# First tokens loaded ahead of the branch, the flag computed first, and the feed-forward normalized a step earlier

## The chip, the cores and the metric

The kernel runs on one core of a Trainium2 chip. The metric is the device time of one execution in microseconds. Before the change it is 2756.72 us, the median of three executions (2755.34 to 2758.24).

The core has five instruction queues that matter here: TensorE (PE in the profile, its weight loads PEld), VectorE (DVE), ScalarE (ACT), GpSimd (POOL) and SyncE (SP), which here does nothing but issue DMAs. Each works through its instructions in the order of the program and waits at semaphores.

## What is computed

The input `x` has the shape (2, 256, 128, 128): batch, time, band, channel. A block of three residual parts is applied, all in float32:

```python
xt = _ln(x, ln_t_w, ln_t_b).transpose(0, 2, 1, 3)
x = x + _mha(xt, t_wi, t_bi, t_wo, t_bo, H_T, cm).transpose(0, 2, 1, 3)   # over time, causal
xf = _ln(x, ln_f_w, ln_f_b)
x = x + _mha(xf, f_wi, f_bi, f_wo, f_bo, H_F, bm)      # over bands, |i - j| <= 16
xn = _ln(x, ln_n_w, ln_n_b)
h = jax.nn.gelu(xn @ w1.T + b1, approximate=False)     # 512 hidden channels
x = x + (h @ w2.T + b2)
```

`_ln` is a layer norm over the 128 channels, `_mha` an attention of four heads of 32 channels.

## The kernel before

**Prologue.** `load_constants` (L39) issues the loads of the columns of constants and the rows of biases on SP, and the six weights on ACT's DMA queue. `fold` (L335) then folds the layer norms' scales into the weights (`wf`, `w1f`), works out the biases (`bq`, `orow`, `b1`), and computes from the weights' norms a flag that says whether the scores are small enough to take exponentials without subtracting the maximum. Every engine reads the flag (L423) and branches (L1118). `bounded_path` is the branch that is taken here; `shifted_path` is the other. Matmuls of `fold` write to PSUM tiles that one pool holds; VectorE does all the elementwise work. The scheduler orders the instructions of `fold`.

**Groups.** After the branch all work is cut into groups of four tiles of 128 tokens (512 tokens of 128 channels). There are 128 groups of attention over time (`OverTime`), and then sixteen runs, each of 8 groups of attention over bands (`OverBands`) and 8 of the feed-forward (`FeedForward`) on the same tokens. Four groups share a quad, a tile `x` of four DMAs of 256 KB. There are four such buffers. Attention over time writes its sum to a tensor `x1` in DRAM, from which the bands' groups load; the bands' sum stays on the chip as `x2`, where the feed-forward reads it.

**What a group goes through.** `statistics` (mean and variance, on VectorE), a reciprocal root (`rstd`), `normalize` (VectorE writes `xh`, four instructions), `turn` (VectorE transposes 32x32 blocks into `z`, and four DMAs write it to a DRAM tile `turned`), `fetch` (one DMA of 256 KB reads it back as `xnT`, channels on partitions), and then the products. In the attentions these are `qp`, `kp`, `vp`, the scores `sp`, the sums `rp` and `op`, and the output `yp`; in the feed-forward `hp` (four products of 128x512, in two halves) and `zp`.

**The pipeline.** `run` writes one step per group index `n`, and in each step the parts of several groups that are at different stages. `do_at(n + 3, OverTime, "fetch")` says that in step `n` group `n + 3` is fetched if it is one over time. The order of PE, VectorE, ACT and POOL is kept as it is written (`InOrder`); SP's is not, and a scheduler puts its DMAs in order by what it reckons to be ready. The lines that matter:

```python
        for n in range(-11, len(groups) + 2):
            do(n + 11, "load")
            do_at(n + 3, OverTime, "fetch")
            do_at(n + 2, OverBands, "fetch")
            do_at(n + 1, FeedForward, "fetch")
            do_at(n + 2, FeedForward, "normalize", "turn")
            do_at(n + 3, OverBands, "normalize", "turn")
            do_at(n + 4, OverTime, "normalize", "turn")
```

So the bands' groups are normalized three steps ahead and fetched two, the feed-forward's two and one. The tiles `xnT` have three buffers, `xh` and `z` two, `turned` three. The first `load`s stand in eleven steps in which nothing else happens yet; they issue two DMAs of a quad at a time. DMAs share eight semaphores, and one that takes a semaphore waits for the DMA that had it before.

Of the kernel before, what the change touches and what calls it, by code (L numbers as in the profile page):

```python
# [10 lines left out]
F32 = mybir.dt.float32  # L11
# [8 lines left out]
P = 128  # L20
# [18 lines left out]
def load_constants(ctx, tc, x, t_wiT, t_woT, f_wiT, f_woT, w1T, w2T, cols, rows):  # L39
    nc = tc.nc  # L40
    B, T, FB, C = x.shape
    k = Consts()
    k.NI = w1T.shape[1] // P
    const = ctx.enter_context(tc.tile_pool(name="const", bufs=1))
    k.const = const
    k.cols = const.tile([P, 16], F32, name="cols_sb")
    nc.sync.dma_start(k.cols, cols)
    k.rows = const.tile([P, 3, C], F32, name="rows_sb")
    for i in range(3):
        nc.sync.dma_start(k.rows[:, i, :], rows[i : i + 1, :].partition_broadcast(P).squeeze(1))  # L50
# [284 lines left out]
def fold(tc, k):  # L335

    nc = tc.nc
    const = k.const  # L340
    C = P
    scale = 1.0 / math.sqrt(D)

    def col(i):
        return k.cols[:, i : i + 1]
# [3 lines left out]
    k.wf, k.wn, k.bq, k.orow = [], [], [], []  # L349
    tests = const.tile([P, 6], F32, name="tests")  # L350
    with tc.tile_pool(name="foldp", bufs=2) as fp, tc.tile_pool(name="foldps", bufs=1, space=PSUM) as pp:
        for a in range(2):
            c0 = 5 * a
            wi, wo = k.wiT[a], k.woT[a]

            bp = pp.tile([P, 2], F32, name="bp")
            nc.tensor.matmul(bp[:, 0:1], wi[:, 0:C], col(c0 + 1), start=True, stop=True)
            nc.tensor.matmul(bp[:, 1:2], wi[:, 2 * C : 3 * C], col(c0 + 1), start=True, stop=True)
            bq = const.tile([P, 1], F32, name=f"bq{a}")
            nc.vector.tensor_scalar(bq, bp[:, 0:1], col(c0 + 2), scale, ALU.add, ALU.mult)  # L360
            bv = fp.tile([P, 1], F32, name="bv")
            nc.vector.tensor_tensor(bv, bp[:, 1:2], col(c0 + 4), ALU.add)
            wf = const.tile([P, 3 * C], F32, name=f"wf{a}")
            nc.vector.tensor_scalar(wf[:, 0:C], wi[:, 0:C], col(c0), scale, ALU.mult, ALU.mult)
            nc.vector.tensor_scalar(wf[:, C : 3 * C], wi[:, C : 3 * C], col(c0), None, ALU.mult)
            wn = const.tile([P, C], F32, name=f"wn{a}")
            nc.vector.tensor_scalar(wn, wo, -1.0, None, ALU.mult)

            bvb = fp.tile([P, P], F32, name="bvb")
            nc.vector.tensor_scalar(bvb, k.ones, bv, None, ALU.mult)  # L370
            op = pp.tile([P, C], F32, name="op")
            nc.tensor.matmul(op, bvb, wo, start=True, stop=True)
            orow = const.tile([P, C], F32, name=f"orow{a}")
            nc.vector.tensor_tensor(orow, op, k.rows[:, a, :], ALU.add)

            brp = pp.tile([1, P], F32, name="brp")
            nc.tensor.matmul(brp, bq, k.ident, start=True, stop=True)
            br = fp.tile([1, P], F32, name="br")
            nc.vector.tensor_copy(br, brp)
            gq = pp.tile([P, P], F32, name="gq")  # L380
            nc.tensor.matmul(gq, wf[:, 0:C], wf[:, 0:C], start=True, stop=False)
            nc.tensor.matmul(gq, br, br, start=False, stop=True)
            gk = pp.tile([P, P], F32, name="gk")
            nc.tensor.matmul(gk, wf[:, C : 2 * C], wf[:, C : 2 * C], start=True, stop=True)
            gs = fp.tile([P, P], F32, name="gs")
            nc.vector.tensor_copy(gs, gq)
            nc.vector.tensor_tensor(gs, gk, gs, ALU.mult)
            for h in range(H):
                r = slice(h * D, (h + 1) * D)
                nc.vector.tensor_reduce(tests[r, 3 * a : 3 * a + 1], gs[r, r], AX.X, ALU.add)  # L390
            for j, w in ((1, wf[:, 2 * C : 3 * C]), (2, wo)):
                sq = fp.tile([P, P], F32, name="sq")
                nc.vector.tensor_tensor(sq, w, w, ALU.mult)
                nc.vector.tensor_reduce(tests[:, 3 * a + j : 3 * a + j + 1], sq, AX.X, ALU.add)
            k.wf.append(wf)
            k.wn.append(wn)
            k.bq.append(bq)
            k.orow.append(orow)
        b1p = pp.tile([P, k.NI], F32, name="b1p")
        for j in range(k.NI):  # L400
            nc.tensor.matmul(
                b1p[:, j : j + 1], k.w1T[:, j * P : (j + 1) * P], col(11), start=True, stop=True
            )
        k.b1 = const.tile([P, k.NI], F32, name="b1")
        nc.vector.tensor_tensor(k.b1, b1p, k.cols[:, 12 : 12 + k.NI], ALU.add)
        k.w1f = const.tile([P, k.NI * P], F32, name="w1f")
        nc.vector.tensor_scalar(k.w1f, k.w1T, col(10), None, ALU.mult)

        tp = pp.tile([P, 6], F32, name="tp")
        nc.tensor.matmul(tp, k.ones, tests, start=True, stop=True)  # L410
        ok = fp.tile([P, 6], F32, name="ok")
        for a in range(2):
            nc.vector.tensor_scalar(
                ok[:, 3 * a : 3 * a + 1], tp[:, 3 * a : 3 * a + 1], SAFE * SAFE / (C * (C + 1)), None, ALU.is_le
            )
            nc.vector.tensor_scalar(
                ok[:, 3 * a + 1 : 3 * a + 3], tp[:, 3 * a + 1 : 3 * a + 3], LARGE, None, ALU.is_le
            )
        allok = fp.tile([P, 1], F32, name="allok")
        nc.vector.tensor_reduce(allok, ok, AX.X, ALU.min)  # L420
        flag = const.tile([P, 1], I32, name="flag")
        nc.vector.tensor_copy(flag, allok)
    return nc.values_load(flag[0:1, 0:1], min_val=0, max_val=1)  # L423


# [451 lines left out]
class BoundedPath:  # L877
# [53 lines left out]
    def groups(self, x, out):  # L931
# [3 lines left out]
        for b in range(B):  # L935
            for f0 in range(0, FB, GA):
                held = {}


                def load(g, f0=f0, b=b, held=held):  # L940
                    if g == 0:
                        self.quad(held, "x", 4)
                    for i in range(2 * g, min(2 * g + 2, NT)):
                        f = f0 + i // NC_T * NT
                        nc.sync.dma_start(held["x"][rows_of(i)], self.of_times(x[b], i, slice(f, f + NT)))

                def store(g, f0=f0, b=b, held=held):
                    for i in range(NT if g % 2 else 0):
# [14 lines left out]
        for b in range(B):  # L963
            for r0 in range(0, T, RUN):
                run = []
                for t0 in range(r0, r0 + RUN, GB):
# [3 lines left out]
                    def load(g, t0=t0, b=b, held=held):  # L970
                        if g == 0:
                            self.quad(held, "x", 4)
                            self.quad(held, "x2", 2 * RUN // GB)
                        for i in range(2 * g, min(2 * g + 2, NT)):
                            nc.sync.dma_start(
                                held["x"][rows_of(i)].rearrange("q g t c -> q (g t) c"),
                                self.of_bands(k.x1[b], t0 + NT * i, NT),
                            )
# [18 lines left out]
                for g, part, _, store in run:  # L997
                    yield FeedForward(self, partial(part, "x2", g), partial(part, "res", g), None, partial(store, g))

    def run(self, x, out):  # L1000
        groups = list(self.groups(x, out))

# [12 lines left out]
        A = RUN // NT  # L1015

        self.scalar.preload_act_table_set(EXP_SET)
        for n in range(-11, len(groups) + 2):
            feeds = [at(n - 2 + i, FeedForward) for i in range(5)]
            bands = [at(n - 2 + i, OverBands) for i in range(5)]  # L1020
            turn = feeds[2] and bands[1]
            old, new = (groups[i] if at(i, OverTime) else None for i in (n, n + 1))
            self.by_columns = at(n - 1, Attention)
            do(n + 11, "load")
            if bands[2] and feeds[1]:
                self.scalar.preload_act_table_set(EXP_SET)
            do_at(n + 4, FeedForward, "root")
# [131 lines left out]
```

## Time and profile before

| | |
|---|---|
| median of three executions | 2756.72 us |
| the profiled execution | 2757.78 us |
| its span, first to last instruction | 2755.9 us |
| granted TensorE clock, mean | 0.997 |
| PE idle at the start, up to 40.88 us | 3.45, 1.49 and 25.77 us |
| PE idle after its last matmul | 8.1 us |
| DMA, mean over the span | 125 GB/s |

Busy time says how long an engine worked; a wait says for what it stood idle and how long. In a row of the timeline the numbers are the start in us from the span's start, the time to the end of the last instruction of the row, the engine, the line, the operation, the tile it writes and what it reads, and the idle time before it with what ended it. Almost every instruction has the line L872, that of the helper that records it, so rows are told apart by their tiles. A matmul of float32 stands as two records. An `issue` row of SP (SPq) is the time that the issuing took, not that of the transfer.

The stretches of the start, in the view by windows (busy us and instructions of each engine, granted clock, share of the DMA engines' time, GB/s):

```profile
0.00:16.50 16.50, 10.18 (x38) 8.01 (x38) 8.81 (x46) 0.00 (x0) 0.69 (x6) 1.00 0.25 76
16.50:23.50 7.00, 0.00 (x0) 0.00 (x0) 0.06 (x1) 1.28 (x1) 0.79 (x3) 1.00 0.87 199
23.50:41.00 17.50, 0.12 (x1) 0.15 (x1) 12.07 (x56) 1.51 (x6) 0.00 (x0) 1.00 0.91 202
```

In the first the fold runs, in the second all engines stand while the DMA engines are 87% busy, in the third VectorE alone works.

### The profile page before, as it was taken

Reading aid. Unit: us, or ns where it says so; the run is one execution under the profiler, and the core shown is the slowest. Engines: PE = TensorE matmul, PEld = TensorE weight load, DVE = VectorE, ACT = ScalarE, POOL = GpSimd, SP = SyncE. Lnnn points to the kernel's source line nnn. Section 1 sums busy time; section 2 is a strip of 40 time slices with the busy share of each in tenths; the row PEclk is TensorE's granted clock in tenths of the full one; section 3 lists DMA queues with packets and bytes.
Section 4 is the critical chain, followed back from the end, with each engine's and each line's share of the span. In section 5 each row is a group of like instructions: output and inputs, shape, how many; then the busy total and the mean of one; then the engine's idle time right before and its main releaser. Section 6 shows DMA issues by size and latency. Waiting matters only on the chain.

```text
span 2755.9 us, 105739 instructions
## 1 busy us (share of the span) xinstructions
PE 2695.7 (98%) x43522; PEld 1880.6 (68%) x43522; DVE 2288.9 (83%) x6727; ACT 1843.3 (67%) x3600; POOL 1861.0 (68%) x2169
## 2 busy tenths in 40 slices
PE   5999999999999999999999999999999999999998
PEld 3666766667666666676676766766766767667666
DVE  5999999999999987868778778687687796776874
ACT  3888888888888874655746646557456465465563
POOL 2878878788887876666657566666566665665762
PEclk9999999999999999999999999999999999999999
DMA  5565555555555564444443544544444445344333
GB/s 126 135 154 135 148 156 141 142 154 144 148 149 144 134 157 105 109 129 108 121 127 105 129 108 109 132 115 115 129 107 122 111 114 130 103 117 113 87 97 86
DMA packets 471310, 343.84 MB, mean 125 GB/s; under 512 B 43296, under 2 KB 405152, under 8 KB 470816
## 3 DMA queue, kind: packets, MB, share of 16 engines
q1 hardware_dynamic: 469568, 335.92, 47.3%
q8 instruction: 344, 5.64, 0.9%
q14 instruction: 150, 1.23, 0.2%
q10 hardware_dynamic: 1248, 1.05, 0.1%
HBM read 169.03 MB, written 167.77 MB: 122 GB/s over the span
## 4 chain that ended last, share of the span: by engine, by line
PE 82%; DVE 11%; DMA 4%; issue 1%; SPq 1%; POOL 1%; ACT 0%; DVEq 0%
PE zp L872 17%; PE hp L872 16%; PE sp L872 10%; PE op L872 7%; PE rp L872 7%; PE vp L872 7%; PE qp L872 6%; PE kp L872 6%; PE yp L872 6%; DVE xh L872 2%; DVE vy L872 2%; DMA xnT<-turned 2%; DVE u L872 1%; DVE stats L872 1%; DVE res L872 1%
## 5 line engine op out<-in xcount | busy, mean ns | idle before, releaser
L872 ACT ACTIVATE hT<-hp,b 128x512 f32<-128x512 f32 x512 | 350.2, 687 | 553.0 <-PE hp L872 542.1
L872 POOL TENSOR_SCALAR_AFFINE_SELECT pf<-pf 128x512 f32<-128x512 f32 x768 | 476.9, 635 | 274.8 <-ACT pf L872 248.6
L872 DVE TENSOR_SCALAR xh<-x,mv,rstd 128x160 f32<-128x160 f32 x1536 | 596.2, 430 | 14.1
L872 PEld LDWEIGHTS zp<-w2T_sb,hT 128*128 128x128 f32 x4096 | 476.3, 192 | 56.2 <-issue 54.1
L872 PE MATMUL hp<-xnT,w1f 128*128 128x512 f32 x1024 | 471.2, 597 | 13.5 <-DMA xnT<-turned 11.6
L872 PE MATMUL zp<-w2T_sb,hT 128*128 128x128 f32 x4096 | 479.8, 275 | 0.1
L872 ACT ACTIVATE p<-sp 128x512 f32<-128x512 f32 (+1 forms) x1024 | 417.3, 501 | 19.9 <-PE sp L872 7.5
L872 POOL TENSOR_SCALAR_AFFINE_SELECT p<-p 128x1024 f32<-128x1024 f32 x256 | 280.2, 1095 | 199.9 <-ACT p L872 199.8
L872 PE MATMUL sp<-qT,kT 32*128 32x128 f32 (+1 forms) x8192 | 363.0, 310 | 5.4 <-DVE oT L872 3.6
L872 PEld LDWEIGHTS sp<-qT,kT 32*128 32x128 f32 x8192 | 310.7, 185 | 56.7 <-ACT kT L872 44.4
L872 PEld LDWEIGHTS vp<-wf,xnT 128*32 128x32 f32 (+1 forms) x7400 | 237.9, 113 | 153.8 <-issue 137.8
L872 POOL TENSOR_TENSOR p<-p,p 128x512 f32<-128x512 f32 x256 | 328.7, 1284 | 10.7
L872 DVE BATCH_NORM_STATS2 stats<-x 128x6 f32<-128x128 f32 x1536 | 327.6, 276 | 6.9 <-DMA x<-in_x 6.8
L872 PEld LDWEIGHTS hp<-xnT,w1f 128*128 128x128 f32 x1024 | 182.3, 191 | 191.4 <-issue 115.3
L872 ACT ACTIVATE pf<-sp 128x512 f32<-128x512 f32 x512 | 264.3, 603 | 59.2 <-PE sp L872 59.0
L872 PE MATMUL qp<-xnT,wf 128*32 128x512 f32 (+1 forms) x1850 | 267.2, 593 | 27.8 <-DMA xnT<-turned 25.8
L872 DVE STREAM_TRANSPOSE z<-xh 128x512 f32<-128x512 f32 x384 | 273.3, 712 | 15.6 <-DMA turned<-z 2.2
L872 POOL TENSOR_SCALAR rstd<-mv 128x4 f32<-128x4 f32 x248 | 56.3, 227 | 331.9 <-DVE mv L872 330.8
L872 ACT ACTIVATE qT<-qp,bq 128x512 f32<-128x512 f32 x256 | 176.0, 687 | 146.0 <-PE qp L872 146.0
L872 PE MATMUL vp<-wf,xnT 128*32 128x128 f32 (+1 forms) x7400 | 272.3, 273 | 0.0
L872 POOL TENSOR_TENSOR rstd<-rstd,mhalf 128x4 f32<-128x4 f32 x248 | 256.6, 1035 | 20.7
L872 PE MATMUL yp<-wn,oT 128*32 128x128 f32 (+1 forms) x7808 | 270.5, 273 | 0.0
(95 smaller groups left out, 4025.3 us busy)
## 6 DMA issues: line engine op xcount, KB each, us to landing
turned<-z SPq DMA_DIRECT2D x1536, 64.0 KB, 2.0
xnT<-turned SPq DMA_DIRECT2D x384, 256.0 KB, 2.8
x<-in_x SPq DMA_DIRECT2D x128, 256.0 KB, 5.4
x<-res SPq DMA_DIRECT2D x256, 128.0 KB, 3.5
x<-x SPq DMA_DIRECT2D x128, 256.0 KB, 4.2
out<-res SPq DMA_DIRECT2D x256, 128.0 KB, 2.4
w1T_sb<-in_w1T ACTq DMA_DIRECT2D x1, 256.0 KB, 4.3
w2T_sb<-in_w2T ACTq DMA_DIRECT2D x1, 256.0 KB, 4.7
```

What stands on the lines that cost most here:

```text
L872: return self.tc.keep_in_program_order(emit(*args, **kwargs))
```

## The change

Five things are changed.

1. The first quad of tokens has a tile of its own, `x0`, and its four loads are issued on SP in `load_constants`, behind the constants and in front of the branch. The first `load` of the first batch then does nothing.
2. `fold` is written anew, with its instructions kept in order. What the flag needs comes first, and part of it is done by ScalarE (copies out of PSUM, and the sums of squares by an activation that accumulates). What it doesn't need (`wn`, `orow`, `w1f`, `b1`) comes after the flag, still in front of the branch.
3. Loads are staggered: each `load` issues one DMA and not two, twelve steps ahead and not eleven, and those of the second to fourth quad are put at steps of their own.
4. Eight products into unused banks (`warm`) are put at the start of the branch.
5. The feed-forward is normalized three steps ahead and fetched two, as the bands are.

```diff
+    k.x0 = const.tile([P, NT, NT, C], F32, name="x0")
+    for i in range(NT):
+        f = i // (T // P) * NT
+        nc.sync.dma_start(k.x0[rows_of(i)], BoundedPath.of_times(x[0], i, slice(f, f + NT)))
...
+    tensor, vector, scalar = InOrder(tc, nc.tensor), InOrder(tc, nc.vector), InOrder(tc, nc.scalar)
...
+        scalar.preload_act_table_set(EXP_SET)
+
+        bp = pp.tile([P, 4], F32, name="bp", tag="small")
+        for a in range(2):
+            tensor.matmul(bp[:, a : a + 1], k.wiT[a][:, 0:C], col(5 * a + 1), start=True, stop=True)
         for a in range(2):
             c0 = 5 * a
...
+            wf = const.tile([P, 3 * C], F32, name=f"wf{a}")
+            vector.tensor_scalar(wf[:, 0:C], k.wiT[a][:, 0:C], col(c0), scale, ALU.mult, ALU.mult)
+            vector.tensor_scalar(wf[:, C : 3 * C], k.wiT[a][:, C : 3 * C], col(c0), None, ALU.mult)
             bq = const.tile([P, 1], F32, name=f"bq{a}")
...
+        brp = [pp.tile([1, P], F32, name=f"brp{a}") for a in range(2)]
+        for a in range(2):
+            tensor.matmul(brp[a], k.bq[a], k.ident, start=True, stop=True)
+
+        for a in range(2):
+            wf, wo = k.wf[a], k.woT[a]
             br = fp.tile([1, P], F32, name="br")
...
+            scalar.copy(br, brp[a])
+            gk = pp.tile([P, P], F32, name="gk", tag=f"gk{a}")
+            tensor.matmul(gk, wf[:, C : 2 * C], wf[:, C : 2 * C], start=True, stop=True)
+            gq = pp.tile([P, P], F32, name="gq", tag=f"gq{a}")
+            tensor.matmul(gq, wf[:, 0:C], wf[:, 0:C], start=True, stop=False)
+            tensor.matmul(gq, br, br, start=False, stop=True)
             gs = fp.tile([P, P], F32, name="gs")
...
+            scalar.copy(gs, gk)
+            vector.tensor_tensor(gs, gq, gs, ALU.mult)
...
+                scalar.activation(sq, w, AF.Square, accum_out=tests[:, 3 * a + j : 3 * a + j + 1])
         tp = pp.tile([P, 6], F32, name="tp")
...
+        for a in range(2):
+            c0 = 5 * a
+            wn = const.tile([P, C], F32, name=f"wn{a}")
+            scalar.mul(wn, k.woT[a], -1.0)
+            k.wn.append(wn)
+
+            tensor.matmul(bp[:, 2 + a : 3 + a], k.wiT[a][:, 2 * C : 3 * C], col(c0 + 1), start=True, stop=True)
+            bv = fp.tile([P, 1], F32, name="bv")
+            scalar.activation(bv, bp[:, 2 + a : 3 + a], AF.Identity, bias=col(c0 + 4))
+            bvb = fp.tile([P, P], F32, name="bvb")
+            scalar.activation(bvb, k.ones, AF.Copy, scale=bv)
+            op = pp.tile([P, C], F32, name="op", tag=f"gk{a}")
+            tensor.matmul(op, bvb, k.woT[a], start=True, stop=True)
+            orow = const.tile([P, C], F32, name=f"orow{a}")
+            vector.tensor_tensor(orow, op, k.rows[:, a, :], ALU.add)
+            k.orow.append(orow)
+        k.w1f = const.tile([P, k.NI * P], F32, name="w1f")
+        scalar.activation(k.w1f, k.w1T, AF.Copy, scale=col(10))
+        b1p = pp.tile([P, k.NI], F32, name="b1p", tag="gq0")
...
                 def load(g, f0=f0, b=b, held=held):
+                    if b == f0 == 0:
+                        held["x"] = k.x0
+                        return
                     if g == 0:
                         self.quad(held, "x", 4)
-                    for i in range(2 * g, min(2 * g + 2, NT)):
-                        f = f0 + i // NC_T * NT
-                        nc.sync.dma_start(held["x"][rows_of(i)], self.of_times(x[b], i, slice(f, f + NT)))
+                    f = f0 + g // NC_T * NT
+                    nc.sync.dma_start(held["x"][rows_of(g)], self.of_times(x[b], g, slice(f, f + NT)))
...
+    def warm(self):
+        for _ in range(8):
+            bank = self.bank([P, 3 * P], "warm")
+            self.tensor.matmul(bank, self.k.ones, self.k.wf[0], start=True, stop=True)
...
-        for n in range(-11, len(groups) + 2):
+        self.warm()
+        for n in range(-12, len(groups) + 2):
...
-            do(n + 11, "load")
...
             do_at(n + 3, OverTime, "fetch")
-            do_at(n + 2, OverBands, "fetch")
-            do_at(n + 1, FeedForward, "fetch")
+            do_at(n + 2, (OverBands, FeedForward), "fetch")
+
+            for i in (2 * n + 12, 2 * n + 13) if n < -2 else (n + 10,) if n < 2 else ():
+                if i >= NT:
+                    do(i, "load")
+            if n < -8 or n >= 0:
+                do(n + 12, "load")
             do_at(n + 5, OverTime, "statistics")
-            do_at(n + 2, FeedForward, "normalize", "turn")
-            do_at(n + 3, OverBands, "normalize", "turn")
+            do_at(n + 3, (OverBands, FeedForward), "normalize", "turn")
             do_at(n + 4, OverTime, "normalize", "turn")
```

The bands' `load` is cut to one DMA in the same way.

More of the change, by code (lines that the diff above doesn't have):

```diff
@@ L351, in fold @@
     with tc.tile_pool(name="foldp", bufs=2) as fp, tc.tile_pool(name="foldps", bufs=1, space=PSUM) as pp:
+        scalar.preload_act_table_set(EXP_SET)
+        bp = pp.tile([P, 4], F32, name="bp", tag="small")
+        for a in range(2):
+            tensor.matmul(bp[:, a : a + 1], k.wiT[a][:, 0:C], col(5 * a + 1), start=True, stop=True)
         for a in range(2):
             c0 = 5 * a
-            wi, wo = k.wiT[a], k.woT[a]
-            bp = pp.tile([P, 2], F32, name="bp")
-            nc.tensor.matmul(bp[:, 0:1], wi[:, 0:C], col(c0 + 1), start=True, stop=True)
@@ L358, in fold @@
-            nc.tensor.matmul(bp[:, 1:2], wi[:, 2 * C : 3 * C], col(c0 + 1), start=True, stop=True)
+            wf = const.tile([P, 3 * C], F32, name=f"wf{a}")
+            vector.tensor_scalar(wf[:, 0:C], k.wiT[a][:, 0:C], col(c0), scale, ALU.mult, ALU.mult)
+            vector.tensor_scalar(wf[:, C : 3 * C], k.wiT[a][:, C : 3 * C], col(c0), None, ALU.mult)
             bq = const.tile([P, 1], F32, name=f"bq{a}")
-            nc.vector.tensor_scalar(bq, bp[:, 0:1], col(c0 + 2), scale, ALU.add, ALU.mult)
@@ L361, in fold @@
[L361 to L377, printed above, removed]
-            br = fp.tile([1, P], F32, name="br")
@@ L379, in fold @@
[L379 to L384, printed above, removed]
+            vector.tensor_scalar(bq, bp[:, a : a + 1], col(c0 + 2), scale, ALU.add, ALU.mult)
+            k.wf.append(wf)
@@ new lines, in fold @@
+            k.bq.append(bq)
+        brp = [pp.tile([1, P], F32, name=f"brp{a}") for a in range(2)]
[3 more added lines that the diff above has]
+            wf, wo = k.wf[a], k.woT[a]
+            br = fp.tile([1, P], F32, name="br")
+            scalar.copy(br, brp[a])
[4 more added lines that the diff above has]
+            tensor.matmul(gq, br, br, start=False, stop=True)
@@ L385, in fold @@
             gs = fp.tile([P, P], F32, name="gs")
-            nc.vector.tensor_copy(gs, gq)
-            nc.vector.tensor_tensor(gs, gk, gs, ALU.mult)
+            scalar.copy(gs, gk)
+            vector.tensor_tensor(gs, gq, gs, ALU.mult)
             for h in range(H):
-                r = slice(h * D, (h + 1) * D)
-                nc.vector.tensor_reduce(tests[r, 3 * a : 3 * a + 1], gs[r, r], AX.X, ALU.add)
+                r = rows_of(h)
+                vector.tensor_reduce(tests[r, 3 * a : 3 * a + 1], gs[r, r], AX.X, ALU.add)
@@ L391, in fold @@
             for j, w in ((1, wf[:, 2 * C : 3 * C]), (2, wo)):
                 sq = fp.tile([P, P], F32, name="sq")
[L393 to L407, printed above, removed]
+                scalar.activation(sq, w, AF.Square, accum_out=tests[:, 3 * a + j : 3 * a + j + 1])
         tp = pp.tile([P, 6], F32, name="tp")
-        nc.tensor.matmul(tp, k.ones, tests, start=True, stop=True)
+        tensor.matmul(tp, k.ones, tests, start=True, stop=True)
@@ L411, in fold @@
         ok = fp.tile([P, 6], F32, name="ok")
         for a in range(2):
-            nc.vector.tensor_scalar(
+            vector.tensor_scalar(
                 ok[:, 3 * a : 3 * a + 1], tp[:, 3 * a : 3 * a + 1], SAFE * SAFE / (C * (C + 1)), None, ALU.is_le
             )
-            nc.vector.tensor_scalar(
+            vector.tensor_scalar(
                 ok[:, 3 * a + 1 : 3 * a + 3], tp[:, 3 * a + 1 : 3 * a + 3], LARGE, None, ALU.is_le
@@ L419, in fold @@
         allok = fp.tile([P, 1], F32, name="allok")
-        nc.vector.tensor_reduce(allok, ok, AX.X, ALU.min)
+        vector.tensor_reduce(allok, ok, AX.X, ALU.min)
         flag = const.tile([P, 1], I32, name="flag")
-        nc.vector.tensor_copy(flag, allok)
+        vector.tensor_copy(flag, allok)
+        for a in range(2):
[16 more added lines that the diff above has]
+        b1p = pp.tile([P, k.NI], F32, name="b1p", tag="gq0")
+        for j in range(k.NI):
+            tensor.matmul(b1p[:, j : j + 1], k.w1T[:, j * P : (j + 1) * P], col(11), start=True, stop=True)
+        k.b1 = const.tile([P, k.NI], F32, name="b1")
+        vector.tensor_tensor(k.b1, b1p, k.cols[:, 12 : 12 + k.NI], ALU.add)
     return nc.values_load(flag[0:1, 0:1], min_val=0, max_val=1)
@@ L973, in load @@
                             self.quad(held, "x2", 2 * RUN // GB)
[L974 to L978, printed above, removed]
+                        nc.sync.dma_start(
+                            held["x"][rows_of(g)].rearrange("q g t c -> q (g t) c"),
+                            self.of_bands(k.x1[b], t0 + NT * g, NT),
+                        )
                     def store(g, t0=t0, b=b, held=held):
```

## The prediction

> **What bounds the kernel now.** First the page's rows of busy time, to see which engine sets the pace; then the waits of TensorE alone, because a full engine can only be made shorter where it still stands idle; then the timeline around those waits.
>
> ```profile
> PE 2695.7 (98%) x43522; PEld 1880.6 (68%) x43522; DVE 2288.9 (83%) x6727; ACT 1843.3 (67%) x3600; POOL 1861.0 (68%) x2169
> ...
> PE qp L872 <- DMA xnT<-turned: 25.8, 1, 25.8
> PE hp L872 <- DMA xnT<-turned: 11.6, 14, 2.1
> ```
>
> PE is busy 2695.7 of 2755.9 us and the change removes no matmul of the main loops. So at most the 60 us of idle time and some cold clock are to be had. The second row is the start: one wait of 25.8 us for the first normalized tokens. The third is fourteen short waits, 11.6 us in all, of `hp`, the feed-forward's first product; its longest is 2.1 us. (What else there is, a 3.6 us wait of `sp` at 985 us and about 8 us after the last matmul, no line of the diff touches.)
>
> The timeline of the start:
>
> ```profile
> 15.75 0.15 DVE L422 CAST flag<-allok 128x1 int32<-128x1 f32 x1
> ...
> 16.63 11.82 SPq L945 DMA_DIRECT2D x<-in_x  x16
> ...
> 23.59 0.87 DVE L872 BATCH_NORM_STATS2 stats<-x 128x6 f32<-128x128 f32 x4 [6.85 <-DMA x<-in_x]
> ...
> 28.56 0.71 DVE L872 STREAM_TRANSPOSE z<-xh 128x512 f32<-128x512 f32 x1
> ...
> 29.37 4.07 SPq L514 DMA_DIRECT2D turned<-z  x4
> ...
> 38.23 0.34 SPq L519 DMA_DIRECT2D xnT<-turned  x1
> ...
> 40.88 2.05 PE L872 MATMUL qp<-xnT,wf 128*128 128x512 f32 x2 [25.77 <-DMA xnT<-turned]
> ```
>
> The flag is ready at 15.90, the loads leave at 16.63, VectorE has its tile turned at 29.27, but the round trip through DRAM ends only at 40.88: `turned` is issued by 33.44 and landed at about 38.2. Ahead of it in SP's queue stand sixteen loads of 256 KB. The loads took from 16.63 to about 37.8 us (the last, issued at 28.1, needed 9.7 us): 2 us of latency and 1.2 us each. So the start is bound by DMA, not by VectorE.
>
> A turn from bands to feed-forward, the first of sixteen:
>
> ```profile
> 1029.37 0.69 DVE L872 TENSOR_TENSOR sp<-sp,band 128x512 f32<-128x512 f32 x1
> ...
> 1036.22 1.60 DVE L872 TENSOR_SCALAR xh<-x,mv,rstd 128x160 f32<-128x160 f32 x4
> ...
> 1038.60 1.76 SPq L514 DMA_DIRECT2D turned<-z  x4
> ...
> 1041.74 0.34 SPq L519 DMA_DIRECT2D xnT<-turned  x1
> ...
> 1045.37 3.67 PE L872 MATMUL hp<-xnT,w1f 128*128 128x512 f32 x8 [0.79 <-DMA xnT<-turned]
> ```
>
> From `xh` to the landed `xnT` it takes 9.1 us (1036.22 to about 1045.3), and PE asks for it 8.2 us after `xh`. VectorE skipped a normalization in the step before (from 1029.37 to 1036.22 there is no `xh`).
>
> **Part 1, the feed-forward one step earlier.** The first `hp` of the sixteen runs starts at 1045.37 and, last, at 2687.28: 109.46 us a run. The runs whose `hp` waits under 0.1 us take 108.4 to 108.5 us. So lateness costs 15 x (109.46 - 108.42) = 15.6 us, and 1.0 in the first run: **16.6 us**. The terms agree: 11.6 us of waits; 0.9 at 2166.85, which the waits put down to VectorE but which again ends as an `xnT` lands; some 0.12 us of drained pipeline at each; and 1.8 us at 2358.73, where the wait of 2.1 us was followed by `hp` taking 5.37 instead of 3.60 us. There a rule can be weighed. Rows: in 2360 to 2362 us the granted clock was 0.50 after that wait. The Trainium skill, "TensorE: Matmul & The Clock Gate", part 1, says the clock halves after an idle window of about 3.4 us. By the row a wait of 2.1 us, after a last stretch of short matmuls, can cost 1.8; by the rule it costs nothing. I take the row.
>
> With `normalize` at n+3 and `fetch` at n+2, `xnT` is issued one step (6.4 us in the bands, 7.0 in the feed-forward) earlier. The longest wait is 2.1 us, so all go. What is late next? VectorE: it does the work that it skipped, four `xh` (1.64 by starts) and a transpose (0.63), 2.27 us, where it now idles 0.66 and 1.09 us. It ends 0.5 us later. Behind it stand `rp`, `u`, `oT` of that step, and PE's `yp` waits for `oT`: `oT` ends at 1034.52 and `yp` starts at 1037.08. In the run that had no wait (`hp` at 2137.38) the tightest is `oT` at 2149.76 before `yp` at 2150.90, 1.1 us. So 0.5 us is covered; without that cover it would cost 16 x 0.5 = 8 us. At a run's end a normalization goes away where two stood in one step; PE waits for neither.
>
> New wait: `xnT` has three buffers, so the fetch of n+2 waits for the last `hp` of n-1. Queued behind it on SP are the next `turned` and stores; it is over at the start of step n, two steps before use. Nothing. The `out` stores move behind one `turned` on SP, also nothing: PE waits for none. I take **16** (bounds 9 and 17).
>
> **Part 2, the start.** The flag's chain, from durations of before: `cols` and `t_wiT` at 3.42; `bp` 0.56, `bq` 0.21 for both (f_wiT by 4.4 us) to 5.2; two `brp`, 5.9; `gk`, `gq` at 0.43 each and `br` through ACT, whose table load (1.28) runs from 4 or 5 us; `gq` of the second at 8.6; product 0.3, four reductions 0.75, `tp` 0.6, tests 0.7, flag: about **11.1** instead of 15.9. But what was put behind the flag stands before the branch on PE, ACT and DVE. After `tp` at 10 us: `bp` 0.55, `bv` and `bvb` on ACT 0.7, `op` 0.8, the same again, then `b1p` 1.87 (four weight loads): about 15.6, and DVE's `b1` ends at 15.8. So DVE branches at the old time, 16.5. Its tokens are there (four loads of `x0` issued from about 3.3 us), and it skips the 6.85 us wait: `z` at 22.2 instead of 29.27. That is 7 us for VectorE, not for PE.
>
> SP branches at 11.9. Its first load writes where the fold's tiles lay and waits for the second `op`: 14.1. That is 2.5 us before 16.63. Then, in the program's order on SP, stand **thirteen** loads, `turned` of the first group, three loads, three `turned`, and only then its `xnT`. The staggering by steps is undone here by the order in which SP holds them. Sixteen loads are still in front of the first `xnT`; they are of the next four quads instead of the first. Sum: 14.1 + 2 + 16 x 1.2 = 35.3; seven `turned` of 64 KB at the same rate, some 1.5, by the row 0.4 for four; `xnT` itself 1.2: 37.3 to 38, against 40.88. Gain **3**.
>
> Row and rule here: the Trainium skill, "DMA: Bandwidth & Descriptors", section on queues, rings and completion order, says that a ring is consumed in order; the 8 us of the first `turned` behind the loads shows it. If instead `turned` and `xnT` could pass the loads, `qp` would follow `z` by 2.3 + 2.6 us, at 28: a gain of 13. I take the row. Lower bound: `op` or the weights late behind 1 MB of `x0` (at 1.2 us per 256 KB, 4.8 us) undo the 2.5: 0 or a loss of 1.
>
> `warm`: eight 128x384 products. By the start's rows a 128x512 cold took 1.7 and warm 0.86 us by starts; 384 columns are 1.3 and 0.65, with 3 cold: 7 us, from 16.3 to 23. Then 14 us idle. The same page's rule speaks against it: after 3.4 us idle the clock falls, and in this trace `qp` at 40.88 is cold after 25.8 us. So `warm` earns 0; had it held, `qp` to `sp` (4.8 us from 40.88) would be about 2 us shorter. It hides wholly in the wait.
>
> **Sum.** The profiled execution took 2757.78 us (span 2755.9, 1.9 around it), 1.1 above the median of 2756.72. 2757.8 - 16 - 3 = **2738.8**; from the median one us less. I say 2738.5.
>
> **Rivals.**
> A, another wait takes half of the feed-forward's gain (VectorE at the turn: `yp` on `oT`, or the 3.33 us reciprocal). For it: VectorE is busy 6.36 of 6.5 us in steps with statistics. Against: the run without a wait went by with 1.1 us spare. 2757.8 - 8 - 3 = 2747.
> B, the start gains 8 to 13, because loads leave SP's way faster and `xnT` finds a warm PE: 2730. For it: VectorE is ready 7 us earlier. Against: sixteen loads at 1.2 us.
> C, slower: SP, one queue in order, meets the fetch that waits for a buffer while the next `turned` stands behind it, and each feed-forward step loses instead. It decides once the fetch is held over 5 us into a step; at 0.3 us for each of 128 feed-forward steps 38 us are lost, less 19: 2777. Against: SP issues one `xnT` (0.34), four `turned` (1.76) and half of the time four stores (2.0), 4 us of a 7 us step at most.
> D, it doesn't do what it says: feed-forward's waits remain since the scheduler keeps `xnT` late: start alone, 2755. Against: the program's order has the first `xh` of each run ahead of a whole step's statistics.
>
> **Chances.** Forecast 0.74 (2734 to 2743.5), A 0.11, B 0.07, C 0.04, D 0.04. The range 2732 to 2747 leaves out C, D, half of B and part of A. A measurement here can tell 0.2%, 5.5 us: faster 0.92, same 0.05, slower 0.03.
>
> **What will show it.** Right: `hp <- DMA xnT` gone from the waits or under 1 us, runs at 108.4 to 108.6 us, no clock of 0.5 at a turn; DVE's first `stats` at 16.5, `qp` at 37 to 39 and still cold, its wait for `xnT` still the one large row. Wrong: `qp` before 34 us (rings not as I count), runs over 109 us with `yp` or `hp` waiting for DVE, or waits of `turned` for SP in the feed-forward.

## The result, and the profile after

| | before | after |
|---|---|---|
| median of four executions | 2757.11 us | **2744.97 us** (2742.98 to 2746.11) |
| the profiled execution | 2757.78 us | 2745.46 us |
| its span | 2755.9 us | 2743.7 us |
| first `qp` | 40.88 us | 38.14 us |
| first `hp` of the first run | 1045.37 us | 1042.41 us |
| from there to the first `hp` of the last run | 1641.91 us | 1631.03 us |
| a run, mean of fifteen | 109.46 us | 108.74 us |
| from that last `hp` to the end of the span | 68.6 us | 70.3 us |

The ratio after to before is 0.9956, with the 95% interval 0.9939 to 0.9973. The time lies 6.5 us above the forecast of 2738.5. It is inside the stated range of 2732 to 2747, but outside the band of 2734 to 2743.5 that was given a chance of 0.74, and nearer to rival A's 2747 than to the forecast. The rows of the table are one sum. The span is 12.2 us shorter: 2.96 before the runs, 10.88 in them, and 1.6 lost after the last `hp`.

The waits of TensorE after the change, longest total first; the columns are the total in us, the count and the longest:

```profile
PE qp L883 <- DMA xnT<-turned: 14.2, 4, 12.6
PE rp L883 <- DVE u L883: 4.3, 16, 0.4
```

The wait of `hp` for `xnT` (11.6 us before) is gone from the list. In its place stands a row that before did not have: `rp`, the attention's sums, waits for VectorE's `u`, once in each of the sixteen runs. The wait at the start has halved, but so has its room: PE is busy with other work up to 25.5 us now.

The timeline of the start after the change:

```profile
13.04 0.15 DVE L883 CAST flag<-allok 128x1 int32<-128x1 f32 x1
...
16.30 8.15 SPq L958 DMA_DIRECT2D x<-in_x  x13
...
18.06 7.50 PE L883 MATMUL warm<-wf,ones 128*128 128x384 f32 x16 [0.35 <-DVE b L883]
...
18.68 0.87 DVE L883 BATCH_NORM_STATS2 stats<-x 128x6 f32<-128x128 f32 x4
...
23.64 0.71 DVE L883 STREAM_TRANSPOSE z<-xh 128x512 f32<-128x512 f32 x1
...
25.27 3.83 SPq L525 DMA_DIRECT2D turned<-z  x4
...
29.91 2.59 SPq L958 DMA_DIRECT2D x<-in_x  x3
33.08 1.28 SPq L525 DMA_DIRECT2D turned<-z  x3
...
34.46 0.39 SPq L530 DMA_DIRECT2D xnT<-turned  x1
...
38.14 2.04 PE L883 MATMUL qp<-xnT,wf 128*128 128x512 f32 x2 [12.58 <-DMA xnT<-turned]
```

The order is the forecast one (thirteen loads, four `turned`, three loads, three `turned`, then `xnT`), but most times in front of it are about 2 us late. `z` is ready at 24.35, and `xnT` is issued only 10 us later.

The view by windows of the same stretch (us, busy time and instructions of PE, PEld, DVE, ACT and POOL, granted clock, DMA share, GB/s):

```profile
18.00:26.00 8.00, 7.50 (x16) 4.01 (x16) 6.51 (x37) 1.12 (x5) 0.00 (x0) 1.00 1.06 237
26.00:30.00 4.00, 0.00 (x0) 0.00 (x0) 3.86 (x18) 0.39 (x2) 0.00 (x0) 0.89 1.07 239
30.00:42.00 12.00, 3.86 (x6) 1.83 (x7) 1.76 (x4) 0.76 (x2) 0.00 (x0) 0.50 0.82 207
```

The DMA engines are full up to 30 us and 82% busy in the last stretch. The clock that `warm` bought is gone before `qp` starts: 0.50 from 30 us on.

The turn of the first run in the timeline, PE's and VectorE's rows:

```profile
1040.93 1.60 DVE L883 TENSOR_SCALAR xh<-x,mv,rstd 128x160 f32<-128x160 f32 x4
...
1042.41 3.70 PE L883 MATMUL hp<-xnT,w1f 128*128 128x512 f32 x8
...
1045.53 0.69 DVE L883 SCALAR_TENSOR_TENSOR u<-rp,r 128x512 f32<-128x512 f32 x1
...
1046.37 1.07 PE L883 MATMUL rp<-pf,ones 128*32 128x512 f32 x8 [0.26 <-DVE u L883]
```

`hp` starts without a wait. Every step has its `xh` now; the one that VectorE used to skip stands two steps earlier, at 1027.87. `u` ends at 1046.22, and PE's `rp` starts 0.15 us later. What ties them is a bank of PSUM, the memory that products are written to: the kernel gives its eight banks out by turns, and the bank that `rp` gets here holds the sums of the step before, which VectorE's own `rp` (its product of these sums) and `u` still read. Experiment 4 tests this.

### The profile page after: what moved, and what is told of

Same layout as the page of the kernel before. It is cut to its first block, busy times and chain, and to the rows that moved or that the text cites. A ratio compares the mean times of both kernels' runs of the same rounds, so it can differ in the third digit from the quotient of the medians.

```text
span 2743.7 us, 105794 instructions
## 1 busy us (share of the span) xinstructions
PE 2700.1 (98%) x43538; PEld 1886.4 (69%) x43538; DVE 2281.1 (83%) x6708; ACT 1847.8 (67%) x3620; POOL 1861.0 (68%) x2169
## 4 chain that ended last, share of the span: by engine, by line
PE 66%; DVE 24%; DMA 6%; issue 2%; SPq 1%; POOL 0%; ACT 0%; ACTq 0%; DVEq 0%
PE zp L883 17%; PE hp L883 14%; PE sp L883 7%; PE op L883 5%; DVE xh L883 5%; PE rp L883 5%; PE vp L883 5%; PE qp L883 5%; PE kp L883 5%; PE yp L883 4%; DVE stats L883 3%; DVE u L883 3%; DVE rp L883 3%; DMA xnT<-turned 2%; DVE vy L883 2%
## 5 line engine op out<-in xcount | busy, mean ns | idle before, releaser
L883 DVE TENSOR_SCALAR xh<-x,mv,rstd 128x160 f32<-128x160 f32 x1536 | 596.7, 430 | 14.1
L883 DVE TENSOR_TENSOR res<-zp,res 128x512 f32<-128x512 f32 x128 | 87.4, 683 | 236.5 <-PE zp L883 236.5
```

The costliest lines, as they stand in the source:

```text
L883: return self.tc.keep_in_program_order(emit(*args, **kwargs))
```

## The experiments

All ran on the same kind of chip beside executions of before: 2755.88 us (median of 15) for the first four, 2755.68 (7) for the next four, 2756.26 (7) for the last. Times below are medians, spans and rows are from the profiled execution of each. Where a time is compared with after's 2744.97, note that before itself was 2757.11 us beside after: counted from the before beside each, the gains over after are 1.2 us smaller in experiment 4, 1.4 in 5 to 8 and 0.9 in 9. Where such a difference is given, the smaller figure stands behind it, marked "by the befores".

**1. Part 5 alone.** Before, with the feed-forward's `normalize` and `fetch` moved and nothing else:

```diff
-            do_at(n + 2, OverBands, "fetch")
-            do_at(n + 1, FeedForward, "fetch")
+            do_at(n + 2, (OverBands, FeedForward), "fetch")
...
-            do_at(n + 2, FeedForward, "normalize", "turn")
-            do_at(n + 3, OverBands, "normalize", "turn")
+            do_at(n + 3, (OverBands, FeedForward), "normalize", "turn")
```

> The kernel before with the fifth part alone: the feed-forward normalized three steps ahead and fetched two. Theory (the two parts add, and the feed-forward gives 11 to 12 us): runs of 108.7 us instead of 109.5, no wait of hp for xnT, a wait of rp for VectorE's u of 0.25 us in each of the sixteen runs; qp first at 40.9 us as before; total 11 to 12.5 us below before. Rival (part of the feed-forward's gain comes only because the start shifts the phase of the loads): runs over 109 us or hp waits left; 6 to 9 us below before.

Measured: 2745.70 us (ratio 0.9966, 0.9952 to 0.9980), runs of 108.69 to 108.78 us. PE's waits:

```profile
PE qp L872 <- DMA xnT<-turned: 26.4, 2, 25.9
PE rp L872 <- DVE u L872: 4.1, 16, 0.3
```

The new wait belongs to this part: it is there, sixteen times, with the old prologue and the old start. 10.2 us are gained, a little under the 11 to 12.5 expected, and the greater part of the change.

**2. The start alone.** After, with the lines of experiment 1 put back as they were.

> The changed kernel without its fifth part: the feed-forward is normalized two steps ahead and fetched one, as before. Theory (the start is worth 2.7 us at qp, of which some is lost again in the attention over time): qp first at 38.1 us, hp's waits for xnT as before (10 to 13 us), runs of 109.3 to 109.6 us, total 0 to 3 us below before. Rival (the staggered loads help the feed-forward's fetches too): runs under 109.2 us and 5 us or more below before.

Measured: 2752.03 us, ten executions (ratio 0.9986, 0.9976 to 0.9995); first `qp` at 38.07, runs of 109.37 us on the mean. In its waits `rp` is no longer listed, and `hp` is back:

```profile
PE hp L883 <- DMA xnT<-turned: 12.2, 16, 1.5
```

3.9 us are gained where 0 to 3 were expected; the runs are in the expected range. 10.2 and 3.9 are 14.1, against 12 for the whole; each of these differences is uncertain by 3 to 4 us.

**3. No `warm`.** After, without the eight products.

```diff
-        self.warm()
```

> The changed kernel without the eight products at the start of the branch. Theory (they end 12.6 us before qp, and the clock has fallen again by then): qp first at 38.1 us within 0.3, from qp to the first sp 5.1 us as with them, time the same within 1 us. Rival (they hold a part of the clock, or cost DMA or instruction time): from qp to sp under 4 us with them only, so 1 us or more longer without; or qp earlier without them.

Measured: 2744.39 us (ratio 0.9963, 0.9949 to 0.9977), first `qp` at 38.16, second at 45.13 (after: 45.50), runs of 108.73 on the mean. `warm` is worth nothing here that these runs can tell from zero.

**4. Another bank at the turn.** After, with the turn's `rp` written to the bank of the attention's `qp`, which no instruction uses at that point.

```diff
-        self.rp = path.bank([P, NT * P], "rp")
+        self.rp = path.bank([P, NT * P], "rp", path.held.pop("qp") if path.turning else None)
+        if path.turning:
+            path.turn_of_bank()
...
-            turn = feeds[2] and bands[1]
+            turn = self.turning = feeds[2] and bands[1]
```

> The changed kernel, but in the first feed-forward step of a run rp is put into the bank that is held for qp and not used there; all other banks stay. Theory (rp waits for VectorE's u only because it gets the bank that the rp of the step before had, which u reads): the wait of rp for u gone, runs of 108.4 us instead of 108.7, 4 to 5 us less than the changed kernel. Rival (VectorE is the bound at the turn, and another instruction will wait for it, such as yp for oT): rp's wait gone, but yp, op or hp wait 0.2 us or more in each run, and the total is within 1.5 us of the changed kernel.

Measured: 2740.45 us (ratio 0.9947, 0.9930 to 0.9963), 4.5 us less than after (3.3 by the befores). Thirteen of fifteen runs take 108.37 or 108.38 us, the mean is 108.40. PE's part of the turn, and VectorE's `u` in it:

```profile
1041.71 3.70 PE L885 MATMUL hp<-xnT,w1f 128*128 128x512 f32 x8
...
1044.81 0.69 DVE L885 SCALAR_TENSOR_TENSOR u<-rp,r 128x512 f32<-128x512 f32 x1
...
1045.34 1.06 PE L885 MATMUL rp<-pf,ones 128*32 128x512 f32 x8
```

From `hp` to `rp` it takes 3.63 us instead of 3.96, `rp` has no wait and starts before `u` has ended (1045.50), and no other wait took its place. VectorE is as late as in after (`u` 3.10 us behind the start of `hp`, there 3.12), so it is the bank and not VectorE's work as such that cost the time.

**5. SP's order.** After, with SP's DMAs of the steps up to n = 1 kept in the order in which the steps write them.

```diff
+        nc_sync = self.nc.sync
...
+            self.sync = InOrder(self.tc, nc_sync) if n < 2 else nc_sync
...
-            path.nc.sync.dma_start(self.turned[:, :, i, :].rearrange("c a x -> a c x"), z[rows_of(i)])
+            path.sync.dma_start(self.turned[:, :, i, :].rearrange("c a x -> a c x"), z[rows_of(i)])
```

The same replacement is made in `fetch` and `load`.

> The changed kernel, but SP's loads, turned and xnT of the first steps are kept in the order in which the steps write them, so that four loads and not sixteen stand before the first xnT is read. Theory (SP's queue in front of xnT sets the start): DVE's first stats at 18.6 us as in the changed kernel, qp at 30 to 32 us instead of 38.1, and 5 to 8 us less in all. Rival (the loads cost their DMA time wherever they stand): qp earlier, but the next qp, or statistics of the second quad, wait for loads, and the total is within 2 us of the changed kernel.

Measured: 2739.71 us (ratio 0.9945, 0.9928 to 0.9962), 5.3 us less than after (3.8 by the befores). SP's queue at the start, and below it PE's rows of that stretch:

```profile
15.99 0.79 SPq L883 DMA_DIRECT2D x<-in_x  x2
24.07 1.77 SPq L883 DMA_DIRECT2D turned<-z  x4
27.31 0.34 SPq L883 DMA_DIRECT2D xnT<-turned  x1
27.69 0.91 SPq L883 DMA_DIRECT2D x<-in_x  x2
...
30.54 2.05 PE L883 MATMUL qp<-xnT,wf 128*128 128x512 f32 x2 [5.03 <-DMA xnT<-turned]
...
38.33 1.13 PE L883 MATMUL qp<-xnT,wf 128*128 128x512 f32 x2 [1.16 <-ACT p L883]
```

Two loads stand in front of the first `turned`, where there were thirteen, and in front of `xnT`, where there were sixteen. The first `qp` comes 7.6 us earlier, the second 7.2, and the first `hp` 6.7 (1035.68). What held the start in after was the order of SP's queue. In the profiled execution, the fastest of the four, the span is 7.6 us shorter; by the medians it is the 5.3 or 3.8.

**6. More warming.** After, with 26 products in `warm` instead of 8, so that PE works until shortly before `xnT` lands. The turn of the banks is set back to where after has it.

```diff
-        for _ in range(8):
+        for _ in range(26):
...
+        self.next_bank = 0
```

> The changed kernel with 26 products at the start of the branch instead of eight, so that they end about 1 us before qp at 38.1 us. Theory (the eight only came too early; the clock falls in idle time): granted clock 1.00 at qp, from qp to the first sp about 3 us instead of 5.1, total 1.5 to 2.5 us less than the changed kernel. Rival (what follows qp is paced by ScalarE's exponentials, not by PE): qp to sp shorter, but the second qp comes no more than 1 us earlier, and so the total gains under 1 us.

Measured: 2741.07 us (ratio 0.9952, 0.9936 to 0.9969), 3.9 us less than after (2.5 by the befores). PE's timeline:

```profile
38.56 1.10 PE L883 MATMUL qp<-xnT,wf 128*128 128x512 f32 x2 [1.26 <-DMA xnT<-turned]
...
43.63 1.12 PE L883 MATMUL qp<-xnT,wf 128*128 128x512 f32 x2 [1.15 <-ACT p L883]
```

The first `qp` is 0.4 us later than in after and takes 1.10 us instead of 2.04, and the second stands 5.07 us behind it instead of 7.36. 1.9 us are gained at the second `qp`, so the rival, which allowed 1, fell. That is most of the 2.5; another 0.9 is the wait of `sp` at 972 to 980 us (2.7 instead of 3.55), which need not be due to the edit.

**7. The rest of the fold behind the branch.** After, with `wn`, `bv`, `orow`, `w1f` and `b1` moved from in front of the branch to two of the empty steps behind it, n = -3 (PE and ScalarE) and n = -2 (VectorE). On PE they stand behind `warm` there.

```diff
-        for a in range(2):
-            c0 = 5 * a
-            wn = const.tile([P, C], F32, name=f"wn{a}")
...
+            if n == -3:
+                self.fold_rest()
+            if n == -2:
+                self.fold_end()
             do_at(n + 2, OverTime, "queries_keys", "take_query", "take_key")
```

> The changed kernel with the part of the fold that the flag does not need (wn, orow, w1f, b1) moved behind the branch, into the steps in which PE and ScalarE stand idle. SP's order stays. Theory (DMA in SP's order bounds qp, and the loads start when the fold's tiles are free): SP's first load at 14 us instead of 16.3, DVE's first stats at 14.3 instead of 18.7, qp at 35.5 to 36.5, so 1.5 to 2.7 us less than the changed kernel. Rival (VectorE is the bound of the start): qp 4 us earlier, at 34.

Measured: 2741.71 us (ratio 0.9952, 0.9935 to 0.9968), 3.3 us less than after (1.8 by the befores). VectorE's first `z`, SP's queue, and PE's first `qp`:

```profile
14.10 8.37 SPq L934 DMA_DIRECT2D x<-in_x  x13
...
19.78 0.71 DVE L859 STREAM_TRANSPOSE z<-xh 128x512 f32<-128x512 f32 x1
...
23.46 4.08 SPq L501 DMA_DIRECT2D turned<-z  x4
28.38 2.73 SPq L934 DMA_DIRECT2D x<-in_x  x3
...
33.02 0.40 SPq L506 DMA_DIRECT2D xnT<-turned  x1
...
36.53 2.08 PE L859 MATMUL qp<-xnT,wf 128*128 128x512 f32 x2 [10.68 <-DMA xnT<-turned]
```

VectorE starts its statistics at 14.83 instead of 18.68 and has `z` at 20.49 instead of 24.35, 3.9 us earlier. `qp` gains 1.6: SP starts 2.2 us earlier and then walks through the same queue, in which `turned` leaves only at 23.46, 3 us after `z`. The theory of the queue held, that of VectorE fell.

**8. Together.** Experiments 4, 5 and 7 in one, with 16 products in `warm`.

```diff
-        for _ in range(8):
+        for _ in range(16):
```

> The changed kernel with all three: SP's first steps in order, the rest of the fold behind the branch, the free bank for rp at the turn; and sixteen products at the start of the branch, so that they end about when xnT comes. Theory (the parts add): qp at 26 to 28.5 us, runs of 108.4 us, total 2728 to 2732 us. Rival (the gains at the start run into the same next wait): qp as early, but the stage over time reaches its pace no earlier than in the kernel with SP's order alone, total 2733 or more.

Measured: 2734.03 us (ratio 0.9924, 0.9908 to 0.9941). The time is above the expected 2728 to 2732. The parts did not add: the second `qp` is at 39.15, later than in experiment 5 (38.33), though `xnT` is issued at 23.31. PE's timeline:

```profile
27.57 0.28 PE L861 MATMUL bpv<-cols_sb,t_wiT_sb 128*128 128x1 f32 x2
...
28.86 0.49 PE L861 MATMUL opr<-t_woT_sb,bvb 128*128 128x128 f32 x2 [0.79 <-ACT bvb L861]
...
29.96 1.41 PE L861 MATMUL b1p<-cols_sb,w1T_sb 128*128 128x1 f32 x8
31.23 2.05 PE L861 MATMUL qp<-xnT,wf 128*128 128x512 f32 x2
```

and ScalarE's at the same place:

```profile
28.11 0.26 ACT L861 ACTIVATE bv<-bpv,cols_sb 128x1 f32<-128x1 f32 x1 [9.52 <-PE bpv L861]
```

`qp` waits for no DMA any more. It stands behind `b1p` in PE's own queue, and the products of the fold's rest stand behind 16 products of `warm`. ScalarE waits 9.5 us for them, with VectorE's next root behind.

**9. The same, untangled.** Experiment 8 with `bpv` in front of `warm`, and 8 products in it again. These are two edits at once; no run shows what each is worth alone.

```diff
+        self.fold_first()
         self.warm()
...
-        for _ in range(16):
+        for _ in range(8):
```

> e8_all with two things changed in the start: the first two products of the fold's rest (bpv), on which ScalarE's share of it waits, stand ahead of the warm products and not behind them, and the warm products are 8 and not 16. Theory (in e8_all the start's parts did not add because PE's own queue held them: 12 us of warm products stood in front of bpv, ScalarE waited 9.5 us for it and VectorE's third group 6.9 us for ScalarE's root): both waits go, the first qp comes at 26 to 27.5 us (xnT issued at 23.3, and 3.2 us from there to qp as in e5_sp_order) instead of 31.23, the second qp at 33.5 to 35 instead of 39.15, and the time is 4 to 5 us under that of e8_all: 2729 to 2730. Rival (the loads of the next quads behind it, DMA, set the pace from there): the first qp comes early, but a qp or sp of the first four groups then waits for xnT or x, and the time is 2732 to 2734, as e8_all.

Measured: **2729.46 us** (2727.38 to 2730.91; ratio 0.9899, 0.9883 to 0.9916), the fastest of all, 26.8 us under before and 15.5 under after (14.7 by the befores). PE's timeline:

```profile
14.54 7.22 PE L861 MATMUL warm<-wf,ones 128*128 128x384 f32 x16
...
25.62 2.08 PE L861 MATMUL qp<-xnT,wf 128*128 128x512 f32 x2 [2.62 <-DMA xnT<-turned]
...
33.71 1.13 PE L861 MATMUL qp<-xnT,wf 128*128 128x512 f32 x2 [1.16 <-ACT p L861]
```

The first `qp` comes 5.6 us earlier than in experiment 8, a little more than expected, and the second 5.4. By the medians 4.6 of it reach the end. In the two profiled executions (spans of 2729.4 and 2729.2) nearly none does: the first `hp` is 1.6 us earlier (1032.44 against 1034.01), since `qp` waits for `xnT` at 202.93 (1.75 us), 613.93 (0.28) and 999.89 (0.47), and at 437.88 (0.56) for an `xnT` and ScalarE's `p` that came together; and 1.3 us more pass after PE's last matmul. So the rival has a part of the truth in it: the loads of later quads take back some of an earlier start. How much is not settled by four executions of each.

## Why the prediction was right, and where it was not

**Right: what bounds the start, and what `warm` is worth.** The forecast had sixteen loads in front of the first `xnT` in SP's queue and `qp` at 37.3 to 38. It came at 38.14, and experiments 5 and 7 show the queue to be the cause. `warm` was put at 0 by the row of before against the hope that the clock lasts; experiment 3 shows 0. (The rule of the idle window named there is that of the page on the clock gate, which part 1 of the prediction names, not of the page on DMA.)

**Right by two errors: the size of that part.** The forecast gain was 3, the measured one 2.74, but the path to it is off, and that the two errors nearly cancel is luck. The flag is ready at 13.19 and not at 11.1, SP's first load leaves at 16.30 and not at 14.1, VectorE starts at 18.68 and not at 16.5. Rows of PE in after show where the flag's 2.1 us went:

```profile
5.70 1.08 PE L883 MATMUL brp<-ident,bq 128*1 128x128 f32 x4 [0.40 <-DVE bq L883]
6.71 0.80 PE L883 MATMUL gk<-wf 128*128 128x128 f32 x2
7.29 0.63 PE L883 MATMUL gq<-wf 128*128 128x128 f32 x2
...
9.73 0.79 PE L883 MATMUL gq<-br 1*128 1x128 f32 x2
```

`brp` starts at 5.70, where 5.2 was reckoned. From there PE works without a gap until 10.52, 4.8 us for what the forecast put between 5.2 and 8.6, which is 3.4: the products of `gk` and `gq` start 0.56 to 0.72 us apart and not 0.43. From the last of them to the flag it takes 2.67, where 2.5 was reckoned. So the term that was too small is PE's own products, not the crossings from engine to engine.

Against that, from SP's first load to `qp` it took 21.8 us where the forecast had 23.2 to 23.9. The loads were reckoned at 2 us and 1.2 each, and the last of before was put at 37.8, with the longest time that any of the sixteen took; it landed at 37.31. In after, loads landed every 1.12 us (the first at 19.57, the thirteenth at 33.02), in before every 1.19 (the first at 20.01, the fifteenth at 36.61). And `xnT` landed 0.34 us behind the last `turned` in front of it, where 1.2 was reckoned. The sum for `turned` and `xnT` passing the loads is also off: 22.2 and 4.9 make 27.1, not 28.

**Wrong: the size of part 1.** The sum had 16 for it. Experiment 1 shows 10.2, and the runs of after take 108.74 us where 108.42 were reckoned. The term that failed is "So 0.5 us is covered". That VectorE would end later was right in kind and nearly in size. In before's run without a wait the turn stands so:

```profile
2137.38 3.68 PE L872 MATMUL hp<-xnT,w1f 128*128 128x512 f32 x8
...
2140.20 0.69 DVE L872 SCALAR_TENSOR_TENSOR u<-rp,r 128x512 f32<-128x512 f32 x1
...
2141.04 1.06 PE L872 MATMUL rp<-pf,ones 128*32 128x512 f32 x8
```

There `u` starts 2.82 us behind `hp`, in after 3.12, so 0.30 later. But the cover was looked for in the wrong step and at the wrong reader. The forecast weighed VectorE's lateness at `oT`, in the step that used to have the gap and at the tightest place of the run without a wait. It lasts beyond that step: two steps later, at the turn, `xh` stands 1.48 us ahead of `hp` (1040.93), where in that run of before it stood 1.78 ahead (2135.60). And the spare 1.1 us lie between `oT` and `yp`, which kept 1.0 of them in experiment 4 (`oT` ends at 1046.23, `yp` starts at 1047.24). PE's `rp` has none: in before `u` ended at 2140.89 and `rp` started 0.15 us later, the same distance as in after. The pair was at its limit already, and it is tied by a bank, which the data's own path from `rp` to `oT` doesn't show. The forecast's own price without cover, sixteen times the lateness, is then 16 x 0.30 = 4.8 us. In the trace of after `rp` waits 4.3 us; experiment 4 takes the bank away, and its fifteen runs are 15 x (108.74 - 108.40) = 5.1 us shorter (4.5 by the medians, 3.3 by the befores).

With the bank free the runs are as forecast: (109.46 - 108.40) x 15 = 15.9, where 15.6 was reckoned.

**Rivals.** A was half right: another wait did take a part of part 1's gain, and VectorE at the turn was its place, though the reader was `rp` and not `yp`. It took 4.3 us of waits and not 8. B did not come in after, but experiment 5 shows that it was to be had: with the loads out of the way `qp` comes at 30.54, 10.3 us before that of before. C and D fell: no wait of the feed-forward for a DMA is left.

**Not foreseen.** In the profiled execution 1.63 us went in waits of `qp` for `xnT` in attention over time (0.68 at 184.42, 0.23 at 214.06, 0.72 at 449.17), which before did not have there; they took most of the 1.0 expected in front of the first run. They need not belong to the change, since of experiments 3 and 4, with the same loads, the one has no such wait and the other one of under 0.2 us. And 9.3 instead of 8.1 us pass after PE's last matmul. In the eleven traces, one of each kernel, that tail lies between 7.6 and 10.3 us; whether it goes with the kernel or with the execution is not shown.

## What to carry to other kernels

When a change makes an engine later, list every instruction that waits for it, by the buffers it frees as well as by the data it makes, and in the steps that follow until the lateness is made up; the spare time of the nearest consumer says nothing about the next user of the same bank. Staggering transfers in the program's text did nothing for the start here, since a scheduler orders the queue that carries them: read the order from the trace, and pin it where the first result stands behind loads that nobody needs yet. And when several fixes of one stage are put together, read the stage anew, since what one of them adds in front of another (here `warm` in front of `bpv`) can undo it.

## What the runs showed of the hardware

**Short products did not hold the clock.** In experiment 9, by windows of half a us (the granted clock is the figure before the last two):

```profile
24.50:25.00 0.50, 0.00 (x0) 0.00 (x0) 0.50 (x5) 0.00 (x0) 0.00 (x0) 1.00 1.03 365
25.00:25.50 0.50, 0.00 (x0) 0.00 (x0) 0.50 (x2) 0.00 (x0) 0.00 (x0) 0.51 1.12 303
```

`warm` ended there at 21.8, six short products (`opr`, `b1p`) at 23.0, and the clock fell at 25.0, after an idle time of 2.0 us. In experiment 7 `warm` ended at 22.7, the short products (with `bpv`) at 25.9, and the clock fell at 27.2, after 1.4 us. In experiment 8 `warm` ended at 27.7 and the clock fell at about 30.3 (0.64 on the mean from 30 to 31), though with short products behind it PE was never idle for more than 0.8 us in between. In after and in experiment 5, where nothing followed `warm` (end at 25.6 and 25.5), it fell at about 29.1 and 29.3. Counted from the end of `warm` these are 3.2, 4.5, 2.5, 3.6 and 3.8 us; counted from the last product of any kind they run from 3.8 down to none. The Trainium skill, "TensorE: Matmul & The Clock Gate", part 1, has the clock halved after an idle window of about 3.4 us. That agrees roughly if products of one column or of 128 columns hardly count as activity, which is a reading of these places and was not tried by itself.

**An idle time of 1.26 us kept the clock** in experiment 6: `qp` took 1.10 us there, against 2.05 behind the 5.03 us of experiment 5. What stood ahead of it were dense products up to 37.3, unlike the short ones ahead of the 1.4 us of experiment 7.

**A granted clock of 1.00 in a view is not always the full clock.** In before and in experiment 3 the view gives 1.00 at the first `qp`, which takes 2.05 us there, as it does in after at 0.50. In after the view gives 1.00 from 18 to 26 us, but the products of `warm`, recorded in two halves each, have halves that start 0.64 us apart up to about 22 us and 0.32 apart from there on. In these traces the figure stands at 1.00 until the first fall that was recorded, so at the start the time of a known product tells the clock, and the figure does not.
